# A graph layer on one core: first edges of the later chunks found in pieces in block 5, second sums added in pairs

## The chip, the cores and the metric

The kernel runs on one core of a Trainium2 chip. The metric is the device time of one execution in microseconds (us), the median of several runs. Engines are called as in the profile: PE is TensorE (PEld its weight loads), DVE is VectorE, ACT is ScalarE, POOL is GpSimd, SP is SyncE, which only issues DMAs. L339 is line 339 of the kernel before.

## The reference

One layer of a graph network on 6250 nodes with 64 features and 206250 edges, sorted by destination. Each node's features are normalized and clipped at zero; each edge's message is its source's row plus the edge's own 64 features; messages are summed by destination; an MLP follows, and the node's input is added.

```python
h = jnp.maximum(_layernorm(x, axis=-1), 0.0)
msg = h[src] + edge_feat                       # 206250 x 64
agg = jax.ops.segment_sum(msg, dst, num_segments=6250)
out = x + relu(agg @ W1 + b1) @ W2 + b2
```

## The kernel before

The two halves of the message are summed in different ways.

**The h half.** `h` is held in SBUF (`h2`). Three nodes make a window; each window takes up to 128 edges. Per window (a "tile"), `count` (L838) makes on PE, from one-hots that DVE prepares (`rows_of_tiles`, L823; every second call begins with `encode`, L808), a table of how often each source occurs for each of the window's nodes; ACT copies it to `ring` (L852). `products` (L858) multiplies `h2` with that table over 49 pieces, and `add_products` (L890) adds the result to the sums `agg` on DVE. Six tiles are a step, 14 steps a block of 84 tiles or 252 nodes; there are 22 blocks and 311 steps. A block's products run in steps 1 to 8 of the next block (`FRESH` is 9), and its sums are added in step 9. Some nodes' windows hold more than 128 edges; 14 further tiles ("second tiles") at the end of block 3 hold the rest. Their results, in `tail`, are added by `add_seconds` (L900) at places that are known only at run time: a group of node numbers is loaded into DVE registers, and then each is added on its own (L907). Once all are in, the MLPs of blocks 0 to 3 become ready (`ready`).

**The edge half.** Edge features are summed by chunks of 42 nodes. A chunk starts at the edge that is its first node's first; `chunk_starts` (L318) finds these with small matmuls (L324), `chunk_rows` (L327) turns them into numbers from which SP's loads take their addresses, `chunk_columns` (L333) adds the starts of four quarters on DVE (L339, `quarters`) and turns them into columns with matmuls against a one (L345), and `chunk_index` (L348) copies these out as a gather's indices. Then, for each group `t` of 32 chunks, POOL gathers the destinations (`fetch_dst`, L359), DVE makes them relative to the chunk (`chunk_nodes`, L363; L367 and L368), and PE and ACT turn them (`chunk_turn`, L371; L375 and L376) into `rel`. From it `chunk_hot` makes one-hots (L418), `chunk_sum` sums the edges into `bank` (L429), and `chunk_place` (L453) adds them to the block's products. There are 132 chunks in 5 groups; groups 0 and 1 are used from the start on, group 2 from block 10 on.

**The last 24 groups of 1024 edges** get their h rows from a table in DRAM: POOL gathers them one column at a time and adds them to the loaded edge features (`pfeat`), in a queue with planned costs (`pool_until`, L975); an urgent gather is put at its head. `features_h` (L981) then sums them.

**Order.** The instructions of each engine stand in the order in which the program issues them: the loop over steps (L1121) first runs what the table `before` (L1016) has for step n, then `count`, the one-hots of the next three steps when n mod 3 is 1, products, sums, second sums, an MLP if one is ready (its hidden layer L934 and L936, its product L942 two steps later, its sum L947 a step after that), and last what `later` and `turns` hold. The codes of the windows are unpacked in four steps (L655 to L674) and turned by `turn` (L680). PSUM tiles with the tag "po" share one buffer: `pstart`, `pcols`, `pdst`, the `pw` of `turn`, `ph` and `po` of the MLPs, and `over` of two checks at step 100 (L769). Each has to wait until the one before it has been read. `dstq`, shared by the gathered destinations and `quarters`, has two.

Until now the later chunks' first edges (chunks 64 to 131) are worked out at steps 64 to 71, where also the second sums are added, at steps 66 to 69 in groups of 4, 4, 4 and 2; the gathers for groups 2, 3 and 4 are issued at steps 72, 76 and 80, made relative 8 steps later and turned 9 steps later.

Of the kernel before, what the change touches and what calls it, by code (L numbers as in the profile page):

```python
# [10 lines left out]
F32 = mybir.dt.float32  # L11
# [11 lines left out]
P = 128  # L23
# [42 lines left out]
NX = 14  # L66
# [3 lines left out]
SB = 3  # L70
ST = 6
STEPS = BT // ST

FRESH = 9
# [12 lines left out]
NC = NS // CN  # L87
CV = CN // V
assert NC * CN == NS and BN % CN == 0 and CV * V == CN and NX == CV
RC = P // JQ  # L90
NT = -(-NC // RC)
# [28 lines left out]
def gnn_kernel(ctx: ExitStack, tc: tile.TileContext, x, src_t, dst_t, dst_g, edge, w1, b1, w2, b2, out):  # L120
# [195 lines left out]
    known = {}  # L316
# [10 lines left out]
    def chunk_rows(c0, c1):  # L327
        px = known.pop(("s", c0))
        s = starts[:, c0:c1]
        nc.vector.tensor_scalar(s, px[:1, :c1 - c0], float(G * P * J - CE), None, op0=OP.min)  # L330
        nc.vector.tensor_copy(starts_i[:, c0:c1], s)

    def chunk_columns(t0, t1, tag="po", bufs=1):  # L333

        px = ps.tile([P, NT + 1], F32, tag=tag, name="pcols", bufs=bufs)
        n = (t1 - t0) * RC
        assert n <= JP * RC
        quarters = late.tile([P, JP * RC, JQ], F32, tag="dstq", bufs=2, name="quarters")[0:1, :n]
        nc.vector.tensor_tensor(quarters, starts[:, t0 * RC:t1 * RC].unsqueeze(2).to_broadcast([1, n, JQ]),  # L339
                                row_e.unsqueeze(1).to_broadcast([1, n, JQ]), op=OP.add)  # L340
        rows = [(t, quarters[:, (t - t0) * RC:(t - t0 + 1) * RC, :]) for t in range(t0, t1)]
        if t0 == 0:
            rows.append((NT, row_n))
        for t, of in rows:
            nc.tensor.matmul(px[:, t:t + 1], of.rearrange("o c q -> o (c q)"), ones[0:1, 0:1], start=True, stop=True)  # L345
        known["t", t0] = px
# [61 lines left out]
    def load(u):  # L408
        for k in range(GB):
            load_chunk(u, k)  # L410
# [476 lines left out]
    hids.append(hots_p[0][:, :BN])  # L887
    spare["hotp"] = [a.rearrange("p (j w) -> p j w", j=J) for a in hots_p]

    def add_products(b):  # L890
        pv = pvs.pop(b)
        n = nodes(b)
        for a, z, c in at_columns(b, 0, n):
            to = agg[:, start[b] + a:start[b] + z]
            nc.vector.tensor_tensor(to, to, pv[:, c:c + z - a], op=OP.add)  # L895
        if b == SB:
            for a, z, c in at_columns(b, n, n + NX * V):
                nc.vector.tensor_copy(tail[:, a - n:z - n], pv[:, c:c + z - a])

    def add_seconds(k):  # L900
        n = min(4, NX - k)
        node = nc.values_load_multi_w_load_instructions(
            second_n[0:1, k:k + n], engines=[mybir.EngineType.DVE], min_val=0, max_val=DUMP,
            skip_runtime_bounds_check_because="sums of a node's number and 0, at most DUMP by a min")[1]
        for j in range(n):
            to = agg[:, ds(node[j], V)]
            nc.vector.tensor_tensor(to, to, tail[:, (k + j) * V:(k + j + 1) * V], op=OP.add)  # L907
# [91 lines left out]
        f()  # L999
    chunk_rows(0, 2 * RC)  # L1000
    load(0)
    chunk_columns(0, 2, "pc", 2)
    turn(0, P, columns(0))
    seek(9, 3)
# [7 lines left out]
    for g in range(GA + 2, GA + 4):  # L1012
# [13 lines left out]
        13: [second_flags],  # L1026
        15: [second_ranks],
        17: [second_words],
        64: [lambda: chunk_starts(2 * RC, NC)],
        68: [lambda: chunk_rows(2 * RC, NC), lambda: chunk_columns(2, NT)],  # L1030
        71: [lambda: chunk_index(2, NT)],
        100: [lambda: outside(0), lambda: outside(1)],
        (NW - 1) * STEPS + 8: [limits],
        (NW - 1) * STEPS + 9: [limits_found],
# [30 lines left out]
    unpack_later(n - 4, lambda: unpack(2 * PC, 1, NX, second_b, NX))  # L1065
    turns.setdefault(n, []).append(lambda: turn(2 * PC, NX, [(0, NX, SX)]))
    for t in range(1, NT):
        n = 18 if t == 1 else 64 + 4 * t
        before.setdefault(n, []).append(lambda t=t: queue.insert(0, (GATHER_US, lambda: fetch_dst(t))))
        n = 32 if t == 1 else n + 8  # L1070
        before.setdefault(n, []).append(lambda t=t: chunk_nodes(t))
        before.setdefault(n + 1, []).append(lambda t=t: chunk_turn(t))
# [48 lines left out]
    for n in range(NSTEP):  # L1121
        b, s = block_of(n)
        for f in before.get(n, []):
            f()
        count(n)
        if n % (HT // ST) == 1 or n == 0:
            rows_of_tiles(n // (HT // ST) + 1) if n else None
        if b and 1 <= s < FRESH:
            products(b - 1, PART[s], PART[s + 1])
        if b and s == FRESH:  # L1130
            add_products(b - 1)
            if b - 1 > SB:
                ready.append(b - 1)
        if b - 1 == SB and s > FRESH and (s - FRESH - 1) * 4 < NX:
            add_seconds((s - FRESH - 1) * 4)
            if (s - FRESH) * 4 >= NX:
                ready[:0] = range(SB + 1)
        if s in (2, 9) and ready:
            mlp(ready.pop(0), n)
        for f in later.pop(n, []) + turns.pop(n, []):  # L1140
            f()
        if n >= 3:
            if s in (5, 11) and h_next < G and fetched.get(min(h_next + 1, G - 1), 1e9) + LAND_US <= clock(n):
                features_h(h_next)
                h_next = min(h_next + GB, G)
                add_later(n + 3)
            if n == 3:
                pool[0] = clock(n - 1) + OPENING_US
            pool_until(clock(n) + LAND_US)
# [144 lines left out]
```

## Time and profile before

| | before |
|---|---|
| median of 3 runs | 504.35 us (502.35 to 505.71) |
| profiled execution | 503.97 us |
| its span, first to last instruction | 502.3 us |
| mean granted PE clock | 0.943 |
| PE busy | 429.1 us (85%) |
| DVE, ACT, POOL busy | 354.3, 351.8, 374.1 us |

The span and the busy times are of the profiled execution. Busy shares are means over stages with different limits; step 64 lies at about 135 us and step 72 at about 150 us of the span, steps 77 to 89 between 157 and 178 us, and steps 97 to 105 between 188 and 203 us.

### The profile page before, as it was taken

Reading aid. Unit: us, or ns where it says so; the run is one execution under the profiler, and the core shown is the slowest. Engines: PE = TensorE matmul, PEld = TensorE weight load, DVE = VectorE, ACT = ScalarE, POOL = GpSimd, SP = SyncE. Lnnn points to the kernel's source line nnn. Section 1 sums busy time; section 2 is a strip of 40 time slices with the busy share of each in tenths; the row PEclk is TensorE's granted clock in tenths of the full one; section 3 lists DMA queues with packets and bytes.
Section 4 is the critical chain, followed back from the end, with each engine's and each line's share of the span. In section 5 each row is a group of like instructions: output and inputs, shape, how many; then the busy total and the mean of one; then the engine's idle time right before and its main releaser. Section 6 shows DMA issues by size and latency. Waiting matters only on the chain.

```text
span 502.3 us, 17233 instructions
## 1 busy us (share of the span) xinstructions
PE 429.1 (85%) x7194; PEld 374.7 (75%) x7195; DVE 354.3 (71%) x776; ACT 351.8 (70%) x517; POOL 374.1 (74%) x260
## 2 busy tenths in 40 slices
PE   3023799998879998999999999999998999999984
PEld 3023688877768788888788888888887888888864
DVE  4799858977588765787758757787666686677721
ACT  3628978687556767768688778778776677677650
POOL 6866848888887788888888888888888888885000
PEclk9556779999989998999999999999998999999998
DMA  8849637587465665857658758659658568567310
GB/s 225 238 130 301 142 72 190 135 198 174 115 154 127 170 148 133 191 139 187 162 119 211 170 127 217 156 122 246 149 134 216 102 148 204 129 154 168 107 38 15
DMA packets 113355, 78.65 MB, mean 157 GB/s; under 512 B 32736, under 2 KB 108632, under 8 KB 113048
## 3 DMA queue, kind: packets, MB, share of 16 engines
q1 hardware_dynamic: 84356, 65.87, 45.0%
q0 software_dynamic: 28624, 10.11, 17.1%
q10 hardware_dynamic: 292, 1.52, 0.9%
q8 instruction: 58, 0.95, 0.8%
q14 instruction: 25, 0.20, 0.1%
HBM read 73.48 MB, written 3.99 MB: 154 GB/s over the span
## 4 chain that ended last, share of the span: by engine, by line
PE 53%; ACT 14%; DVE 11%; POOL 10%; issue 6%; DMA 5%; DVEq 0%; POOLq 0%; ACTq 0%
PE pv L864 20%; PE pc L846 17%; POOL pfeat L283 9%; ACT ring L852 8%; PE bank L429 6%; DMA pfeat<-table,src_p 4%; DVE hot L832 2%; PE bank L486 2%; PE po L942 2%; ACT kq L695 2%; PE pv L459 2%; PE ph L934 1%; ACT kv L699 1%; DMA firsts_i<-in_dst_g 1%; PE pk L688 1%
## 5 line engine op out<-in xcount | busy, mean ns | idle before, releaser
L283 POOL DMA_INDIRECT pfeat<-table,src_p x188 | 325.9, 1734 | 60.7 <-issue 51.5
L852 ACT ACTIVATE ring<-pc 128x882 fp32r<-128x882 f32 x310 | 276.7, 924 | 82.1 <-PE pc L846 70.4
L846 PE MATMUL pc<-hot 128*128 128x147 fp8e4 x1862 | 178.4, 234 | 25.2 <-ACT ring L852 13.5
L832 DVE TENSOR_TENSOR hot<-at,of 128x576 int32<-128x576 bf16 x208 | 163.2, 826 | 41.4 <-PE pc L846 30.6
L864 PE MATMUL pv<-ring,h 128*128 128x252 f32 (+1 forms) x1078 | 171.3, 296 | 0.8 <-ACT ring L856 0.8
L846 PEld LDWEIGHTS <-hot 128*128 128x128 fp8e4 x1862 | 128.7, 101 | 49.4 <-issue 21.8
L864 PEld LDWEIGHTS pv<-ring,h 128*128 128x128 f32 x1078 | 140.5, 192 | 1.2 <-ACT ring L856 1.0
L429 PE MATMUL bank<-feat,hotf 128*18 128x64 f32 x3168 | 73.5, 225 | 3.1 <-issue 2.0
L429 PEld LDWEIGHTS bank<-feat,hotf 128*18 128x18 f32 x3168 | 49.2, 99 | 21.6 <-issue 4.8
L895 DVE TENSOR_TENSOR sums<-sums,pv 128x252 f32<-128x252 f32 (+4 forms) x34 | 10.0, 323 | 52.8 <-PE pv L864 37.6
L418 DVE TENSOR_TENSOR hotf<-rel,iota 128x432 f32<-128x432 bf16 (+1 forms) x67 | 39.8, 595 | 0.0
L695 ACT ACTIVATE kq<-pk 128x512 bf16<-128x512 f32 (+18 forms) x48 | 18.4, 449 | 12.8 <-PE pk L688 10.2
L813 DVE TENSOR_TENSOR at<-iota_a,kq 128x576 bf16<-128x576 bf16 (+1 forms) x52 | 23.5, 452 | 0.5
L936 ACT ACTIVATE after<-ph,b1s 128x252 f32<-128x252 f32 (+3 forms) x26 | 12.0, 469 | 15.3 <-PE ph L934 14.0
L283 POOL DMA_INDIRECT sums<-in_dst_g,row_i x15 | 17.4, 1162 | 7.0 <-issue 4.3
L819 DVE TENSOR_TENSOR of<-of,kv 128x432 bf16<-128x432 bf16 (+1 forms) x52 | 20.0, 385 | 3.3 <-DVE of L813 0.5
L283 POOL DMA_INDIRECT words<-packed,first_i x15 | 17.7, 1181 | 4.6 <-issue 4.0
L947 DVE TENSOR_TENSOR after<-po,after 126x128 f32<-126x128 f32 (+3 forms) x26 | 7.5, 288 | 18.1 <-PE po L942 18.1
L934 PE MATMUL ph<-sums,w1s 128*128 128x252 f32 (+3 forms) x52 | 17.1, 417 | 3.1 <-issue 1.8
L813 DVE TENSOR_TENSOR of<-iota_w,kq 128x432 bf16<-128x432 bf16 (+1 forms) x52 | 19.5, 374 | 0.0
L324 PE MATMUL pstart<-begins,first 128*1 128x9 f32 (+2 forms) x30 | 1.6, 172 | 17.2 <-DVE sums L509 9.3
L942 PE MATMUL po<-w2s,after 128*126 128x64 f32 (+3 forms) x104 | 15.9, 278 | 0.2 <-issue 0.2
(183 smaller groups left out, 315.6 us busy)
## 6 DMA issues: line engine op xcount, KB each, us to landing
feat<-in_edge SPq DMA_DIRECT2D x132, 384.0 KB
pfeat<-in_edge SPq DMA_DIRECT2D x23, 256.0 KB
pfeat<-table,src_p POOLq DMA_INDIRECT x188
out_y<-after SPq DMA_DIRECT2D x23, 63.0 KB
dstn<-in_dst_g SPq DMA_DIRECT2D x1, 1024.0 KB
table<-xl SPq DMA_DIRECT2D x2, 512.0 KB
after<-in_x SPq DMA_DIRECT2D x4, 252.0 KB
packed<-dstn ACTq DMA_DIRECT2D x1, 768.0 KB
```

The lines of the kernel that those rows point to most:

```text
L283: nc.gpsimd.indirect_dma_start(out=rows, out_offset=None, in_=source, in_offset=bass.IndirectOffsetOnAxis(ap=index, axis=0), compute_op=op)
L418: nc.vector.tensor_tensor(hot_of[u][:, :n].rearrange("p c j w -> p (c j) w"), rel[:, c:c + n].rearrange("p c q k -> p (c q k)").unsqueeze( ...
L429: nc.tensor.matmul(bank[q * QP:q * QP + WQ, at:at + D], hot_of[u][:, c, j, :], feats[u][c][:, j, :], start=(k == 0), stop=(k == JP - 1))
L695: nc.scalar.activation(kq[:, q, at:at + n].rearrange("s i k o -> s (i k) o"), pk[:, q, a:a + n].rearrange("s i k -> s (i k)").unsqueeze(2) ...
L813: nc.vector.tensor_tensor(to[:, :n].rearrange("s i k (m o) -> s (i k) m o", o=2), iota_k.rearrange("s (m o) -> s m o", o=2).unsqueeze(1).t ...
L819: nc.vector.tensor_tensor(pairs_of, pairs_of, kv[:, c:c + n].rearrange("s i k o -> s (i k) o").unsqueeze(2) .to_broadcast([P, 2 * n, WE // ...
L832: nc.vector.tensor_tensor(hot[:, :n, c:c + m * A8].rearrange("s i (w a) -> s i w a", a=A8), at[:, o:o + n, k].unsqueeze(2).to_broadcast([P ...
L846: nc.tensor.matmul(pc[:, k, q * K:(q + 1) * K], hot[:, i, :P], hot[:, i, P:P + K], start=True, stop=True)
L852: nc.scalar.activation(to.rearrange("p h (k m) -> p h k m", k=2), pc[:, :, :ST // 2 * K].rearrange("p k (m h) -> p h k m", h=HI), AF.Copy)
L864: nc.tensor.matmul(pvs[b], h2[:, h, :], ring[:, h, c:c + columns_of_block(b)], start=(h == 0), stop=(h == HI - 1))
L934: nc.tensor.matmul(ph[:, :n], w1s, agg[:, start[b]:start[b + 1]], start=True, stop=True)
L942: nc.tensor.matmul(po[:pairs[b], k, :], hid[:, k:2 * pairs[b]:2], w2s, start=True, stop=True)
```

## The change

The later chunks' first edges are worked out 13 steps later and in more pieces: `chunk_starts` at step 77, `chunk_rows` at 79, the quarters (now a function of their own) at 80, the columns' matmuls at 83, the index at 85. The gathers move by 16 steps, to 88, 92 and 96, with what follows them (relative at 96, 100, 104; turned at 97, 101, 105). The second sums are added two at a time in the seven steps 66 to 72. For the first two groups of chunks, in the opening, quarters and columns are still called one after the other.

```diff
-    def chunk_columns(t0, t1, tag="po", bufs=1):
-
-        px = ps.tile([P, NT + 1], F32, tag=tag, name="pcols", bufs=bufs)
+    def chunk_quarters(t0, t1):
         n = (t1 - t0) * RC
         assert n <= JP * RC
         quarters = late.tile([P, JP * RC, JQ], F32, tag="dstq", bufs=2, name="quarters")[0:1, :n]
         nc.vector.tensor_tensor(quarters, starts[:, t0 * RC:t1 * RC].unsqueeze(2).to_broadcast([1, n, JQ]),
                                 row_e.unsqueeze(1).to_broadcast([1, n, JQ]), op=OP.add)
+        known["q", t0] = quarters
+
+    def chunk_columns(t0, t1, tag="po", bufs=1):
+
+        px = ps.tile([P, NT + 1], F32, tag=tag, name="pcols", bufs=bufs)
+        quarters = known.pop(("q", t0))
...
+    SECONDS = [(SB + 1) * STEPS + FRESH + 1 + k for k in range(-(-NX // 2))]
+
...
     def add_seconds(k):
-        n = min(4, NX - k)
+        n = min(2, NX - k)
...
     load(0)
+    chunk_quarters(0, 2)
     chunk_columns(0, 2, "pc", 2)
...
-        64: [lambda: chunk_starts(2 * RC, NC)],
-        68: [lambda: chunk_rows(2 * RC, NC), lambda: chunk_columns(2, NT)],
-        71: [lambda: chunk_index(2, NT)],
+        77: [lambda: chunk_starts(2 * RC, NC)],
+        79: [lambda: chunk_rows(2 * RC, NC)],
+        80: [lambda: chunk_quarters(2, NT)],
+        83: [lambda: chunk_columns(2, NT)],
+        85: [lambda: chunk_index(2, NT)],
...
     for t in range(1, NT):
-        n = 18 if t == 1 else 64 + 4 * t
+        n = 18 if t == 1 else 80 + 4 * t
...
-        if b - 1 == SB and s > FRESH and (s - FRESH - 1) * 4 < NX:
-            add_seconds((s - FRESH - 1) * 4)
-            if (s - FRESH) * 4 >= NX:
+        if n in SECONDS:
+            k = SECONDS.index(n)
+            add_seconds(2 * k)
+            if 2 * k + 2 >= NX:
                 ready[:0] = range(SB + 1)
```

## The prediction

> **What bounds the kernel now.** I read the page first, then the list of waits, then the timelines of TensorE and VectorE around the moved pieces, and last the busy time by stretches.
>
> ```profile
> span 502.3 us, 17233 instructions
> PE 429.1 (85%) x7194; PEld 374.7 (75%) x7195; DVE 354.3 (71%) x776; ACT 351.8 (70%) x517; POOL 374.1 (74%) x260
> ```
>
> TensorE is the fullest engine, and most of its idle time lies in the opening. What a change is worth is therefore the TensorE time that it takes out of the chain or puts into it. The timeline of TensorE shows where the change starts (steps 64 to 72; each group of L846 is one step's count; in brackets stand the idle time before a row and its releaser):
>
> ```profile
> 135.31 0.40 PE L324 MATMUL pstart<-begins,first 128*1 128x10 f32 x10
> ...
> 136.76 0.30 PE L846 MATMUL pc<-hot 128*128 128x147 fp8e4 x2
> ...
> 138.35 0.56 PE L846 MATMUL pc<-hot 128*128 128x147 fp8e4 x6
> ...
> 143.99 0.88 PE L345 MATMUL pcols<-ones,quarters 1*128 1x1 f32 x6 [3.17 <-DVE quarters L339]
> 144.80 0.92 PE L846 MATMUL pc<-hot 128*128 128x147 fp8e4 x6
> ...
> 151.09 0.69 PE L934 MATMUL ph<-sums,w1s 128*128 128x252 f32 x2
> ```
>
> L324 (step 64) is the matmul of the first edges, and L345 (step 68) that of the index columns. L345 stands idle for 3.17 us, because `quarters` on VectorE is queued behind everything in this view:
>
> ```profile
> 139.12 0.44 DVE L895 TENSOR_TENSOR sums<-sums,pv 128x162 f32<-128x162 f32 x2 [3.98 <-PE pc L846]
> ...
> 139.70 0.76 DVE L907 TENSOR_TENSOR sums<-sums,after 128x3 f32 x4
> 140.37 1.57 DVE L832 TENSOR_TENSOR hot<-at,of 128x576 int32<-128x576 bf16 x2
> 141.86 0.74 DVE L907 TENSOR_TENSOR sums<-sums,after 128x3 f32 x4
> 142.52 0.60 DVE L418 TENSOR_TENSOR hotf<-rel,iota 128x432 f32<-128x432 bf16 x1
> ...
> 143.87 0.73 DVE L907 TENSOR_TENSOR sums<-sums,after 128x3 f32 x4
> 145.19 0.36 DVE L907 TENSOR_TENSOR sums<-sums,after 128x3 f32 x2 [0.59 <-issue]
> 145.46 0.45 DVE L813 TENSOR_TENSOR at<-iota_a,kq 128x576 bf16<-128x576 bf16 x1
> ...
> 146.73 1.58 DVE L832 TENSOR_TENSOR hot<-at,of 128x576 int32<-128x576 bf16 x2
> ...
> 148.36 0.68 DVE L926 TENSOR_TENSOR after<-after,b2s 126x512 f32<-126x512 f32 x1
> ```
>
> VectorE itself waited until 139.12 for the products of step 64, and only then works off the sums of block 3, two groups of second sums, the one-hots of steps 67 to 69 and the small pieces. The pause also costs clock, as the busy time by stretches shows (the last three columns are granted clock, DMA share and GB/s):
>
> ```profile
> 141.21:144.63 3.42, 0.64 (x6) 0.64 (x6) 3.14 (x13) 0.91 (x1) 2.83 (x2) 1.00 0.83 226
> 144.63:148.04 3.41, 3.41 (x62) 2.56 (x61) 2.68 (x7) 1.51 (x2) 2.80 (x3) 0.50 0.22 29
> 192.41:195.83 3.42, 1.62 (x20) 1.36 (x16) 0.33 (x1) 3.33 (x9) 2.81 (x3) 1.00 0.51 119
> 195.83:199.24 3.41, 3.41 (x21) 3.32 (x20) 1.77 (x3) 1.51 (x2) 2.88 (x2) 0.50 0.16 14
> 117.32:120.73 3.41, 1.89 (x60) 1.37 (x60) 3.27 (x8) 2.64 (x3) 2.80 (x3) 1.00 0.70 178
> 120.73:124.15 3.42, 3.25 (x57) 2.90 (x58) 3.39 (x7) 2.77 (x5) 3.12 (x2) 1.00 0.85 215
> ```
>
> After a stretch with 0.64 us of TensorE work the next one runs at clock 0.50; so it does after one with 1.62 us, and not after one with 1.89 us. A count takes 0.92 instead of 0.56 us there (144.80 against 138.35), so one such stretch loses about 3.41 x (1 - 0.56 / 0.92) = 1.3 us.
>
> **Term 1, steps 64 to 72.** The change takes L324 and L345 out of this stretch and spreads the second sums over steps 66 to 72. Without L324 everything from step 64 on comes 136.76 - 135.31 = 1.45 us earlier: L895 starts at 137.67. From there the chain is VectorE's. Since an MLP reads sums that any second sum may touch, the hidden layer of block 0 (L934, step 72) now has to wait for the last group, which is issued in step 72 too; before, the last group was over at 145.55, long ahead of 151.09. The chain, by the rows: L895 with its copy 0.58 (139.12 to 139.70); two sums 0.27 (145.19 to 145.46); one-hots 1.49 (140.37 to 141.86); two sums 0.27; L418 0.60; two sums 0.27 (step 68); 0.59 for a register load with nothing ahead of it, and two sums 0.27 (step 69); encoding and one-hots 2.85 (145.46 to 148.31, step 70); two sums 0.27; 0.59 and two sums 0.27 (step 71); L926 0.68 and the last two sums 0.36 (step 72). Together 9.36, so the sums end at 147.03 and L934 starts at about 147.05: **4.0 us earlier** than 151.09. TensorE does not get there first: count 68 would be over at 139.8, its chunk's matmuls wait for L418 until 140.9, count 72 waits for the one-hots until 144.9, and L934 for the sums. One wait of 3.17 becomes three of about 1.1, 0.9 and 0.7, in two stretches, each with over 1.89 us of work left; I take the clock as full. Bounds: seven groups instead of four mean three more loads. If no load showed, TensorE alone would gain another 2.7 (the three waits), 6.7 in all; if all seven showed, five more than I count, the gain would be 4.0 - 5 x 0.59 = 1.1. I take 4.0, since loads that have a long instruction ahead of them (140.37, 143.87) show no idle time in the rows.
>
> **Term 2, the pieces that come back.** L324 returns at step 77, in a stretch dense with products: +1.45. L345 returns at step 83 at full clock: 0.88 x 0.56 / 0.92 = +0.5. The three small VectorE pieces between L418's end (143.12) and 143.87 return at steps 79 and 80, where the node pieces of chunk group 2 have just left; these were longer, so that costs nothing. If that cover were gone it would be 0.75. There is one more wait: `pstart` and the turn's `pw` share one PSUM buffer, so the turn at step 77 has to wait until L330, at the head of step 79, has read `pstart`.
>
> ```profile
> 158.60 0.60 DVE L418 TENSOR_TENSOR hotf<-rel,iota 128x432 f32<-128x432 bf16 x1
> 159.12 1.57 DVE L832 TENSOR_TENSOR hot<-at,of 128x576 int32<-128x576 bf16 x2
> ...
> 159.38 0.31 PE L689 MATMUL pw<-identb,code 128*128 128x128 bf16 x1
> ```
>
> L418 is of step 78 and L832 of step 79, so VectorE is at L330's place at 159.12; the turn's L689 comes at 159.38 and with L324 ahead of it at 160.8. Cost nothing, with 1.6 us to spare.
>
> **Term 3, the transposes.** They go from steps 81, 85, 89 to 97, 101, 105, and their gathers by the same 16 steps on POOL's queue, where nothing but each other waits for them so far from their use in block 10.
>
> ```profile
> 164.09 0.61 PE L375 MATMUL pdst<-shift,dstq 128*128 128x128 f32 x3
> ...
> 175.59 0.61 PE L375 MATMUL pdst<-shift,dstq 128*128 128x128 f32 x3 [0.39 <-DVE after L947]
> ```
> ```profile
> 166.25 0.41 DVE L367 TENSOR_SCALAR dstq<-dstq,cols 128x384 f32<-128x384 int32 x1
> 166.70 0.62 DVE L368 SCALAR_TENSOR_TENSOR dstq<-iota_q,cols,dstq 128x384 f32<-128x384 int16 x1
> ```
>
> Leaving: 3 x 0.44 (0.61 less the overlap with what follows) and the wait of 0.39: -1.7. Arriving, they meet a stretch that is worse:
>
> ```profile
> 186.95 3.42 ACT L852 ACTIVATE ring<-pc 128x882 fp32r<-128x882 f32 x4 [0.50 <-PE po L942]
> ...
> 195.12 0.47 ACT L936 ACTIVATE after<-ph,b1s 128x252 f32<-128x252 f32 x1
> ```
> ```profile
> 187.01 0.29 DVE L947 TENSOR_TENSOR after<-po,after 105x128 f32<-105x128 f32 x1
> 187.21 1.57 DVE L832 TENSOR_TENSOR hot<-at,of 128x576 int32<-128x576 bf16 x2
> ```
> ```profile
> 187.91 0.55 PE L846 MATMUL pc<-hot 128*128 128x147 fp8e4 x6 [0.24 <-issue]
> ...
> 194.39 0.69 PE L934 MATMUL ph<-sums,w1s 128*128 128x252 f32 x2 [1.80 <-issue]
> 194.92 0.55 PE L846 MATMUL pc<-hot 128*128 128x147 fp8e4 x6
> ```
>
> At step 97 the transposes stand ahead of count 97 (187.91) and need the one PSUM buffer that L947 of step 96 frees; L947 now comes 1.03 later (L367 and L368 go ahead of it), ends at 188.33, and with 0.44 of transposes count 97 starts at 188.8: 0.9 late. ScalarE, which is full from 186.95 to 195.59, would take up count 97 at 188.7 and takes it at 189.45: +0.8, and this reaches L934 of step 100, which already waits 1.80 us for ScalarE to free the same buffer. At step 101 the next transposes stand ahead of count 101 (194.92) and must wait for L936's end at 195.59: +0.7 and +0.44. At step 105: +0.44, no wait. Sum **+2.4**. Bounds: 0.4 (only step 105 shows, the rest disappears into the 1.80 us), and 7.2 (three node pieces on VectorE 3.1, transposes 1.3, the two waits 1.5, one more slow stretch 1.3).
>
> The Trainium skill, page "TensorE: Matmul & The Clock Gate", section "Why this matters for your kernels", asks for no TensorE idle gaps above about 3 us between bursts. By that rule 3.17 would cost clock and neither the 1.80 us at step 100 nor anything I add there could. This trace disagrees: 1.80 us of idle time in one stretch was followed by 0.50. By the rule the sum would be the same, since I count that slow stretch before and after.
>
> **The sum.** -4.0 + 1.45 + 0.5 - 1.7 + 2.4 = -1.35. The profiled execution took 503.97 us (502.3 of it the span); it becomes 502.6. It lies 0.38 below the median of the runs shown, so the median becomes 504.35 - 1.35 = **503.0**.
>
> **Rivals.**
>
> *Block 6 hides the transposes.* Term 3's arrivals fall to 0.4, and with the pauses cut up no stretch falls below 1.89 us of work, so that the slow one after 195.83 goes as well: -1.35 - 2.0 - 1.3 = -4.65, 499.7. For it: L934 waits anyway. Against it: the wait is for ScalarE, and the delayed count 97 feeds ScalarE.
>
> *The loads show.* All seven groups pay 0.59: +2.95, 506.0, slower than before. It decides from the third of the five additional loads on (1.35 / 0.59 = 2.3). For it: three more loads, and groups of two leave less work to cover the next. Against it: in steps 66 to 68, 70 and 72 something long stands ahead.
>
> *Block 6 takes it back.* The wait at L375 of step 97 and 101 becomes the bound, with its upper price of 7.2 instead of 2.4: 503.0 + 4.8 = 507.8, slower. It decides from 3.8 us of cost in steps 96 to 102 on. For it: ScalarE's and VectorE's rows there have no gaps, and one slow stretch is already tripped. Against it: VectorE ends that work early, 0.33 us in 192.41 to 195.83.
>
> *The wait does not go.* Step 68's wait may only change its name, from L339 to L418 and L907; that is counted in term 1 and in the loads.
>
> **How the numbers follow.** Forecast 0.43, block 6 hides 0.17, loads show 0.2, block 6 takes it back 0.2. The forecast's own range is 501 to 505. From 499.0 to 507.6 the rivals are in, but for the far half of the last one and what lies beyond the first. About 1%, or 5 us, is what a measurement of this kernel tells from no change. Faster by that needs under 499.3: half of the first rival (0.085) and a twelfth of the forecast, 0.12. Slower by that needs over 509.4: a third of the last rival and a quarter of the one of the loads, 0.12. Within it 0.76.
>
> **What would show it.** Right: no wait of L345 above 0.3 us; L934 of step 72 released by L907, some 4 us earlier; clock 1.00 from 141 to 150; L324 at step 77 taking 1.4 us; L375 at steps 97 and 101 idle 0.5 us or more, released by L947 and L936. Wrong: idle times of 0.59 before most pairs of L907; a slow stretch between 138 and 150; L689 of step 77 waiting; step 101 at the same time as before or later although step 90 came 4 us earlier.

## The result and the profile after

The changed kernel took 507.93 us in the median of 16 runs (504.34 to 510.47), against 501.9 us in the median of the kernel before beside it (16 runs, one of them at 666.24). The ratio is **1.0109, 95% interval 1.0081 to 1.0137**: slower by about 1%, where 503.0 and no change were forecast. The profiled execution took 508.43 us, 506.7 of it the span.

```profile
span 506.7 us, 17240 instructions
PE 432.4 (85%) x7194; PEld 376.5 (74%) x7195; DVE 354.4 (70%) x776; ACT 352.5 (70%) x517; POOL 371.3 (73%) x260
```

The work of the engines is the same, and the span is 4.4 us longer. What the change set out to do did happen. TensorE's timeline in steps 72 to 83 (idle time before a row and its releaser in brackets):

```profile
146.44 0.56 PE L850 MATMUL pc<-hot 128*128 128x147 fp8e4 x6 [0.72 <-DVE hot L836]
...
149.07 0.69 PE L940 MATMUL ph<-sums,w1s 128*128 128x252 f32 x2 [1.08 <-DVE sums L913]
...
155.23 0.55 PE L324 MATMUL pstart<-begins,first 128*1 128x10 f32 x16
155.71 0.56 PE L850 MATMUL pc<-hot 128*128 128x147 fp8e4 x6
...
164.10 0.82 PE L349 MATMUL pcols<-ones,quarters 1*128 1x1 f32 x6 [0.22 <-DVE after L953]
```

The wait of 3.17 us at L345 is gone (L349 waits 0.22), the hidden layer of step 72 (L940) is held by the second sums (L913) as foreseen, and the stretches from 141 on run at clock 1.00:

```profile
141.21:144.63 3.42, 2.81 (x71) 2.08 (x70) 2.66 (x11) 2.92 (x4) 3.11 (x2) 1.00 0.91 247
144.63:148.04 3.41, 2.63 (x34) 2.19 (x31) 2.35 (x8) 3.01 (x4) 2.80 (x3) 1.00 0.96 259
```

Then TensorE's timeline around the transposes' new place (steps 92 to 101):

```profile
180.72 0.45 PE L433 MATMUL bank<-feat,hotf 128*18 128x64 f32 x13 [0.25 <-issue]
...
183.17 0.32 PE L433 MATMUL bank<-feat,hotf 128*18 128x64 f32 x5 [0.49 <-issue]
183.89 0.33 PE L433 MATMUL bank<-feat,hotf 128*18 128x64 f32 x6 [0.41 <-issue]
...
186.29 0.61 PE L379 MATMUL pdst<-shift,dstq 128*128 128x128 f32 x3
...
191.04 0.55 PE L850 MATMUL pc<-hot 128*128 128x147 fp8e4 x6 [1.02 <-issue]
...
195.03 1.21 PE L940 MATMUL ph<-sums,w1s 128*128 128x252 f32 x2 [2.43 <-ACT over L775]
196.80 0.91 PE L379 MATMUL pdst<-shift,dstq 128*128 128x128 f32 x3 [0.56 <-ACT after L942]
197.50 0.95 PE L850 MATMUL pc<-hot 128*128 128x147 fp8e4 x6
```

Three short stops on "issue" (nothing in the profile held TensorE), and a fourth of 0.20 us at 185.35, come ahead of the first transposes, and one of 1.02 us behind them; the wait at step 100, 1.80 before, is 2.43; the transposes of step 101 wait 0.56 for L942 and then take 0.91 instead of 0.61. The busy time by stretches shows why (TensorE's busy time behind the length; granted clock third from the end):

```profile
187.97:191.38 3.41, 2.39 (x29) 2.29 (x27) 2.91 (x6) 1.95 (x4) 2.80 (x3) 1.00 1.08 345
191.38:194.79 3.41, 1.21 (x20) 0.96 (x17) 0.28 (x1) 3.32 (x11) 2.80 (x3) 1.00 0.47 113
194.79:198.20 3.41, 2.61 (x12) 1.85 (x12) 0.00 (x0) 1.91 (x5) 2.80 (x3) 0.50 0.22 19
198.20:201.61 3.41, 3.41 (x21) 3.32 (x19) 2.09 (x3) 1.87 (x3) 2.80 (x3) 0.50 0.17 15
```

Two slow stretches follow, where the kernel before had one.

To place the time I took, from each trace, the moment at which ScalarE starts to read the counts of a step (L856; L852 before), one such moment per step. The table gives the us from one step to another; in brackets stands the number of slow stretches (3.41 us each at a granted clock of 0.50) in steps 96 to 105. Letters name the chips; the first comparison's chip is not known. Kernels marked * were profiled in a run well above their kernel's usual time, and their totals are not used; the ratios leave such runs out, the medians hold every run.

| kernel | chip | 57–73 | 80–96 | 96–105 | 105–126 | 132–150 | 174–204 | span |
|---|---|---|---|---|---|---|---|---|
| before | – | 26.1 | 23.9 | 15.1 (1) | 29.8 | 27.5 | 42.1 | 502.3 |
| after | – | 22.9 | 24.7 | **20.0** (2) | 29.5 | 28.9 | 45.7 | 506.7 |
| c1_pairs_only | A | 24.6 | 24.1 | 13.5 (0) | 30.0 | 26.9 | 42.4 | 501.1 |
| c2_edges_only | A | 22.6 | 23.4 | **17.4** (1) | 29.9 | 26.8 | 43.2 | 501.3 |
| c3_after_checks60 | A | 24.8 | 24.8 | **17.4** (1) | 29.8 | 27.8 | 48.2 | 507.2 |
| c4_before_checks60 | A | 25.0 | 23.4 | 12.9 (0) | 29.9 | 26.9 | 43.2 | 502.6 |
| c0_after_again | B | 22.1 | 21.7 | **19.5** (2) | 27.9 | 26.5 | 41.3 | 492.1 |
| c5_gathers92 | B | 22.1 | 21.8 | 15.4 (1) | 29.9 | 26.5 | 41.3 | 494.1 |
| c6_gathers80_alone | B | 26.2 | 20.7 | **18.1** (1) | 27.9 | 26.5 | 41.3 | 496.7 |
| c7_edges57 * | B | 26.5 | 22.7 | 15.3 (1) | 27.9 | 26.5 | 41.3 | 501.3 |
| d0_before_again * | C | 24.8 | 23.4 | 14.3 (0) | 29.2 | 32.1 | 47.3 | 508.4 |
| d1_gathers92_again | C | 24.9 | 22.0 | 15.1 (1) | 31.5 | 27.2 | 41.8 | 502.6 |
| d2_gathers80_alone_again | C | 26.2 | 21.8 | **16.6** (0) | 29.8 | 26.9 | 42.6 | 504.9 |
| d3_edges57_again | C | 25.7 | 24.0 | 13.5 (0) | 29.8 | 26.9 | 41.8 | 500.1 |
| e0_after_third | D | 23.5 | 24.0 | **18.3** (1) | 29.9 | 28.2 | 43.1 | 503.6 |
| e1_gathers92_third * | D | 24.2 | 22.1 | 15.1 (1) | 32.1 | 30.2 | 41.9 | 507.3 |
| e2_before_half_piece | D | 25.0 | 24.0 | 13.5 (0) | 29.9 | 26.9 | 41.8 | 501.5 |
| e3_after_half_piece | D | 23.6 | 23.5 | **20.5** (2) | 29.6 | 28.9 | 45.0 | 508.0 |
| f0_before_delay10 | B | 24.2 | 23.0 | 13.8 (0) | 30.1 | 26.5 | 41.3 | 489.0 |
| f1_before_delay20 | B | 25.6 | 22.7 | 15.3 (1) | 32.2 | 26.5 | 41.2 | 493.0 |

Bold are the eight kernels with transposes at 97, 101 and 105. In the pair of the first comparison the changed kernel wins 3.2 us in steps 57 to 73, loses 4.9 in 96 to 105, 1.4 in 132 to 150 and 3.7 in 174 to 204. By step 204 it is 8.5 us behind, and by step 310 4.3, since the kernel before has stops of its own in between (1.80 us at 383).

### The profile page after: what moved, and what is told of

It reads as the page before. It is cut to its first block, busy times and chain, and to the rows that moved or that the text cites. A ratio compares the mean times of both kernels' runs of the same rounds, so it can differ in the third digit from the quotient of the medians.

```text
span 506.7 us, 17240 instructions
## 1 busy us (share of the span) xinstructions
PE 432.4 (85%) x7194; PEld 376.5 (74%) x7195; DVE 354.4 (70%) x776; ACT 352.5 (70%) x517; POOL 371.3 (73%) x260
## 4 chain that ended last, share of the span: by engine, by line
PE 67%; ACT 15%; DVE 12%; issue 4%; DMA 2%; DVEq 0%; ACTq 0%
PE pv L868 24%; PE pc L850 22%; ACT ring L856 9%; PE bank L433 8%; DVE hot L836 3%; PE bank L490 3%; PE ph L940 2%; PE po L948 2%; ACT kq L699 2%; PE pv L463 2%; ACT kv L703 1%; DMA feat<-in_edge 1%; PE pk L692 1%; DMA firsts_i<-in_dst_g 1%; DVE xl L541 1%
## 5 line engine op out<-in xcount | busy, mean ns | idle before, releaser
L856 ACT ACTIVATE ring<-pc 128x882 fp32r<-128x882 f32 x310 | 276.8, 924 | 83.8 <-PE pc L850 68.7
L850 PE MATMUL pc<-hot 128*128 128x147 fp8e4 x1862 | 178.4, 234 | 28.0 <-ACT ring L856 15.1
L850 PEld LDWEIGHTS <-hot 128*128 128x128 fp8e4 x1862 | 128.7, 101 | 52.5 <-issue 23.5
L433 PEld LDWEIGHTS bank<-feat,hotf 128*18 128x18 f32 x3168 | 48.8, 98 | 22.6 <-issue 4.3
L699 ACT ACTIVATE kq<-pk 128x512 bf16<-128x512 f32 (+18 forms) x48 | 18.3, 444 | 12.8 <-PE pk L692 10.8
L942 ACT ACTIVATE after<-ph,b1s 128x252 f32<-128x252 f32 (+3 forms) x26 | 12.0, 470 | 17.9 <-PE ph L940 16.2
L817 DVE TENSOR_TENSOR at<-iota_a,kq 128x576 bf16<-128x576 bf16 (+1 forms) x52 | 23.5, 452 | 0.5
L940 PE MATMUL ph<-sums,w1s 128*128 128x252 f32 (+3 forms) x52 | 17.6, 428 | 4.4 <-ACT over L775 2.4
L324 PE MATMUL pstart<-begins,first 128*1 128x9 f32 (+2 forms) x30 | 1.4, 172 | 16.2 <-issue 8.9
```

What stands on the lines that cost most here:

```text
L433: nc.tensor.matmul(bank[q * QP:q * QP + WQ, at:at + D], hot_of[u][:, c, j, :], feats[u][c][:, j, :], start=(k == 0), stop=(k == JP - 1))
L699: nc.scalar.activation(kq[:, q, at:at + n].rearrange("s i k o -> s (i k) o"), pk[:, q, a:a + n].rearrange("s i k -> s (i k)").unsqueeze(2) ...
L817: nc.vector.tensor_tensor(to[:, :n].rearrange("s i k (m o) -> s (i k) m o", o=2), iota_k.rearrange("s (m o) -> s m o", o=2).unsqueeze(1).t ...
L850: nc.tensor.matmul(pc[:, k, q * K:(q + 1) * K], hot[:, i, :P], hot[:, i, P:P + K], start=True, stop=True)
L856: nc.scalar.activation(to.rearrange("p h (k m) -> p h k m", k=2), pc[:, :, :ST // 2 * K].rearrange("p k (m h) -> p h k m", h=HI), AF.Copy)
L940: nc.tensor.matmul(ph[:, :n], w1s, agg[:, start[b]:start[b + 1]], start=True, stop=True)
```

## The experiments

Kernels c1 to c4 ran on chip A, beside 29 runs of the kernel before (503.15 us median). Their expectations set four theories against each other: COLLISION (the moved pieces meet ScalarE's backlog and the one PSUM buffer in steps 96 to 102; in its narrow form, they meet the checks of step 100), LOADS (the register loads of the pairs), SUPPLY (TensorE's instructions come too late there, since the moved matmuls shift what each load of code holds) and SPREAD (node pieces and transposes cost 2 to 4 us in any place there).

**c1_pairs_only**: the kernel before with the second sums in pairs (steps 66 to 72) and nothing else.

```diff
-        n = min(4, NX - k)
+        n = min(2, NX - k)
...
-        if b - 1 == SB and s > FRESH and (s - FRESH - 1) * 4 < NX:
+        if n in SECONDS:
```

> The kernel before with the second sums in pairs at steps 66 to 72; the first edges stay at 64 to 71 and the transposes at 81, 85, 89. Theory COLLISION (the loss arises in steps 96 to 102, where the moved node pieces and transposes meet ScalarE's backlog and the one PSUM buffer): nothing moves there, so no loss; the pairs shorten VectorE's chain ahead of the quarters by four sums, about 0.8 us, but the hidden layer of block 0 waits for the last pair; 1 us faster to 1 us slower than before, and from step 92 to 105 the same pace as before. Rival LOADS (three more register loads and the new wait at step 72 cost the time): 2 to 5 us slower, visible by step 74.

Measured: 503.02 us, ratio 1.001 (0.9981 to 1.0038). The pairs cost and bring nothing that shows. LOADS falls.

**c2_edges_only**: the changed kernel with the sums by fours again (the reverse of the diff above).

> The changed kernel with the second sums again by fours at steps 66 to 69; first edges at 77 to 85, gathers at 88, 92, 96. COLLISION: the whole loss is here, 4 to 7 us slower than before, and it arises between steps 91 and 105; by step 91 it is 3 to 6 us ahead. LOADS: this is faster than before by 3 us or more.

Measured: 507.9 us in 6 runs, which lie at 503 to 506 and at 510 to 511; ratio 1.0103 (1.0053 to 1.0153). So the loss comes with the moved edges and transposes.

**c3_after_checks60** and **c4_before_checks60**: the checks `outside` from step 100 to 60, in the changed kernel and in the one before.

```diff
-        100: [lambda: outside(0), lambda: outside(1)],
+        60: [lambda: outside(0), lambda: outside(1)],
```

> The changed kernel with the two checks of step 100 (outside 0 and 1, 1.3 us of ScalarE, both through the one PSUM buffer) moved to step 60. COLLISION in its narrow form (the checks are what the late transposes collide with): the hidden layer of step 100 no longer waits 2.4 us, no slow clock after it, 4 us or more faster than the changed kernel, about level with before or faster. Rival SUPPLY (TensorE's instructions come too late in steps 92 to 100, since the moved matmuls shift what each load of code holds): still 4 us or more slower than before, with idle times put down to issue at 180 to 192 us. Rival SPREAD (node pieces and transposes cost in any place there): 2 to 4 us slower than before.

> The kernel before with the same two checks at step 60: the control for the last kernel. It has a wait of 1.8 us at step 100 and a slow stretch after it. COLLISION in its narrow form: 2 to 3 us faster than before (1.8 and 1.3 of clock), so that the last kernel has to be compared with this one. SUPPLY and SPREAD: the same wait goes here, 1 to 3 us faster.

Measured: c3 507.34 us, ratio 1.005 (1.0018 to 1.0081); c4 503.78 us, 1.0002 (0.9972 to 1.0032). Without the checks there the changed kernel still needs 17.4 us for steps 96 to 105, and the kernel before 12.9. The checks are at most a part of it, and COLLISION in its narrow form falls. By the ratio c3 lies within SPREAD's 2 to 4 us. Its trace has the stops on "issue" that SUPPLY expected (2.4 us from 178 to 192.5), but c2's has 0.6 and the same 17.4 us. No theory had c4 unchanged; all expected it 1 to 3 us faster.

The next four ran on chip B, beside 35 runs of the kernel before. PLACE is the theory that the transposes' place is the cause; LAG, that being ahead by step 73 is taken back wherever TensorE runs short.

**c0_after_again**: the changed kernel, no edit.

> The changed kernel once more, for a second profile. PLACE (the transposes of L379, now at steps 97, 101 and 105, stand among the checks, the MLP and the sums of block 6, and block 6 pays for them there): 507 to 508.5, with 5 to 8 us lost again between the evacuations of steps 91 and 105, and no loss that comes back in the same place later. LAG (what is won by step 73 puts TensorE ahead of the gathers and of its own instruction stream, and that is taken back at whatever stage is short of supplies): 507 to 508.5 as well, but the loss stands in other places than in the first profile.

**c5_gathers92**: transposes at 109, 113 and 117.

```diff
-        n = 18 if t == 1 else 80 + 4 * t
+        n = 18 if t == 1 else 92 + 4 * t
```

> The changed kernel with the three fetches, rankings and transposes of the later chunks 12 steps later still: transposes at steps 109, 113 and 117, the same places of a block that before had them at (81, 85, 89 are 28 steps earlier), and none of them beside the checks of step 100. PLACE: the loss between steps 91 and 105 falls from 7.7 us to 1 or less, the gain at 81 to 89 stays; 501 to 503. LAG: 4 us or more are lost between steps 91 and 117 all the same; 505 to 508.

**c6_gathers80_alone**: the kernel before with transposes at 97, 101 and 105 and nothing else.

```diff
-        n = 18 if t == 1 else 64 + 4 * t
+        n = 18 if t == 1 else 80 + 4 * t
```

> The kernel before with nothing changed but the fetches, rankings and transposes 16 steps later (transposes at 97, 101, 105); first edges at 64 to 71 and the sums by fours as before. PLACE: no gain at steps 64 to 72, -1.7 us by step 91, then 5 to 8 us lost by step 105; 506 to 509. LAG: nothing is won before, so there is nothing to take back: within 1 us of before at step 105 and in the time, 502 to 504.

**c7_edges57**: the changed kernel with the edges in block 4 and the transposes where they were before.

```diff
-        77: [lambda: chunk_starts(2 * RC, NC)],
-        79: [lambda: chunk_rows(2 * RC, NC)],
-        80: [lambda: chunk_quarters(2, NT)],
-        83: [lambda: chunk_columns(2, NT)],
-        85: [lambda: chunk_index(2, NT)],
+        57: [lambda: chunk_starts(2 * RC, NC)],
+        59: [lambda: chunk_rows(2 * RC, NC)],
+        60: [lambda: chunk_quarters(2, NT)],
+        62: [lambda: chunk_columns(2, NT)],
+        64: [lambda: chunk_index(2, NT)],
...
-        n = 18 if t == 1 else 80 + 4 * t
+        n = 18 if t == 1 else 64 + 4 * t
```

> The changed kernel with the five pieces of the first edges earlier instead of later (steps 57, 59, 60, 62 and 64, in block 4, where no MLP holds the buffer po), and the fetches and transposes where they were before (transposes at 81, 85, 89). Sums in pairs. PLACE: 3 to 4 us are won by step 73 and kept; 499 to 501, the best of all. LAG: won by step 73 and taken back between steps 91 and 105 or later; 503 to 507.

Measured, all beside 497.31 us for the kernel before: c0 496.81, ratio 1.0015 (0.9973 to 1.0057); c5 496.39, 1.0012 (0.9982 to 1.0043); c6 496.76, 1.0015 (0.9978 to 1.0052); c7 494.93, 0.9967 (0.9928 to 1.0005). **On this chip the change costs nothing**, and no theory had foreseen that. Yet in the trace the loss of steps 96 to 105 is there: 19.5 us in c0 and 18.1 in c6, 15.4 in c5.

Two things differ on chip B. TensorE never waits on "issue": after 58 us no row there has more than 0.15 us of it, while such rows add up to 3.5 to 7.4 us in the profiles on A, C and D. The list of TensorE's waits from 100 to 480 us, of the changed kernel in the first comparison:

```profile
PE pc L850 <- ACT ring L856: 7.6, 14, 1.0
PE pc L850 <- DVE hot L836: 3.3, 4, 1.6
PE pc L850 <- issue: 2.4, 6, 1.0
PE ph L940 <- ACT over L775: 2.4, 1, 2.4
PE bank L433 <- issue: 2.0, 6, 0.5
PE bank L490 <- issue: 1.3, 2, 0.9
```

and the same list of c5 on chip B:

```profile
PE bank L490 <- DMA pfeat<-table,src_p: 4.6, 3, 2.2
PE pc L850 <- ACT ring L856: 4.3, 6, 1.0
PE pc L850 <- DVE hot L836: 3.3, 4, 1.6
PE ph L940 <- ACT over L775: 1.8, 1, 1.8
```

And TensorE there catches up with the gathers on POOL, which run one behind the other from 45 us on: near the end it waits for the last of them. TensorE and POOL of c6:

```profile
461.05 0.31 PE L486 MATMUL bank<-after,pfeat 128*64 128x42 f32 x2 [0.38 <-DMA pfeat<-table,src_p]
463.70 0.31 PE L486 MATMUL bank<-after,pfeat 128*64 128x42 f32 x2 [2.34 <-DMA pfeat<-table,src_p]
```
```profile
458.77 2.08 POOL L283 DMA_INDIRECT pfeat<-table,src_p  x1 [0.30 <-issue]
```

In c5, c6 and c7 TensorE waits 2.7 to 4.6 us like this. What is lost around step 100 would then shorten that wait, and the order fits: c5, c6 and c0 need 15.4, 18.1 and 19.5 us for steps 96 to 105 and wait 4.6, 2.7 and 0.2 us for gathers.

The third group ran on chip C (before: 502.94 us, 35 runs). STARVE is the theory that the loss is tied to the chips with "issue" waits and to when TensorE arrives, not to the transposes.

**d0_before_again** (no edit), **d1_gathers92_again**, **d2_gathers80_alone_again** and **d3_edges57_again** (the edits of c5, c6 and c7).

> The kernel before once more, for a second profile of it. The last four kernels ran on a chip where everything took 497 us instead of 503 and no profile showed TensorE idle on 'issue' after the opening; the earlier ones, all at 501 to 508, showed 5 to 7 us of such idle time. STARVE (the idle time called 'issue' belongs to the chip, and the change costs 1% only where it exists): if this chip shows 'issue' waits, 502 to 505 us; if not, 495 to 499 us, and its evacuations then stand within 1 us of the same kernel with late transposes from step 120 on. PLACE (the cost is in the transposes' place, whatever the chip): the same time as the before of this call, and nothing more is expected of it.

> The changed kernel with transposes at steps 109, 113, 117, once more, in the hope of the slower chip. PLACE: no slower than before on either chip (ratio 0.995 to 1.002). STARVE: 1.000 where TensorE shows no 'issue' waits, and 1.005 to 1.012 where it does, as the changed kernel itself, since it is the early arrival and not the transposes that meets those waits.

> The kernel before with the transposes alone at 97, 101, 105, once more. PLACE: slower by 0.8 to 1.2% where the changed kernel is. STARVE: 1.000 (0.997 to 1.003) on either chip, since nothing is won ahead of step 73 that could shift TensorE against its supplies.

> First edges at steps 57 to 64, transposes as before, sums in pairs, once more; its profile there was a disturbed one. PLACE: 0.992 to 0.998 on either chip, the gain of 3 to 4 us kept. STARVE: 0.997 where there are no 'issue' waits (as measured), 1.003 to 1.010 where there are.

Measured: d0 503.38 us, 1.0008 (0.9983 to 1.0033); d1 502.97, 1.0013 (0.9984 to 1.0041); d2 505.26, **1.0049 (1.0021 to 1.0077)**; d3 505.18, 1.0056 (1.0029 to 1.0084). d1 and d2 speak for PLACE against STARVE: moved alone, the transposes lose half a per cent (less than the 0.8 to 1.2% that PLACE had, more than STARVE's 0.3%), and moved on to 109 they lose nothing that shows, though being ahead by step 73 is kept; LAG, which expected no change from d2's edit and a loss from that of c5 and d1, falls. d3 speaks against PLACE and lies in STARVE's range (1.003 to 1.010): it should have won 3 to 4 us and lost half a per cent. Its profiled execution took 501.78 us, so the trace doesn't hold that loss, but it shows that the edges won nothing in block 4 (25.7 us for steps 57 to 73): TensorE waits there for the turn of step 56 to leave the same PSUM buffer.

```profile
126.41 0.54 PE L324 MATMUL pstart<-begins,first 128*1 128x10 f32 x16 [2.70 <-ACT kv L703]
```

The fourth group ran on chip D (before: 503.27 us, 31 runs).

**e0_after_third** (the changed kernel), **e1_gathers92_third** (c5's edit), and **e2_before_half_piece** and **e3_after_half_piece**: the kernel before and the changed one, with 128 more instructions in TensorE's program.

```diff
         px = ps.tile([P, GN], F32, tag=tag, name="pstart", bufs=bufs)
+        for i in range(64 if c0 == 0 else 0):
+            nc.tensor.matmul(px[:1, 0:1], onesb[:, 0:1], onesb[:, 0:1], start=True, stop=True)
```

> The changed kernel, beside its version with later transposes on the same chip. PLACE: 1.008 to 1.012 where 'issue' waits show, 1.000 to 1.003 where not. STARVE: the same; this run is the yardstick for the next three.

> Transposes at steps 109, 113, 117. PLACE: 0.6% or more below the changed kernel of this call wherever that one is slow. STARVE (the place of the transposes is not it): within 0.3% of it.

> The kernel before with 64 more 1x1 bf16 products on TensorE (128 instructions with their weight loads) ahead of its first pstart products, where TensorE waits 9.3 us for VectorE, so that every later instruction stands 128 places further in TensorE's program, half of a 16 KB piece at 64 bytes each. Their results are overwritten. PLACE: the same time as before within 0.3%, the 1.8 us stalls in the same steps. STARVE: the stalls move to other steps, and the time moves by 0.4 to 1% one way or the other where 'issue' waits show; nothing where they don't.

> The changed kernel with the same 128 instructions ahead. PLACE: as slow as the changed kernel of this call, within 0.3%. STARVE: its loss changes by 0.4% or more, since the stalls fall elsewhere than at 180 to 195 us.

Measured: e0 508.04 us, **1.0091 (1.0056 to 1.0126)**; e1 506.03, 1.0014 (0.9973 to 1.0055); e2 502.87, 0.9991 (0.9959 to 1.0022); e3 508.24, 1.0065 (1.0025 to 1.0104). The loss repeats on a second chip. The shift of the program moves neither kernel by more than its interval, so STARVE and SUPPLY, as places in the program, find no support. Beside e0, the later transposes of e1 take most of the loss away by the ratio; by the medians it is 2 of the 4.8 us, and e1's 12 runs lie anywhere from 500.4 to 509.0, so the size stays loose. In d1 and e1 the transposes cost some 2 us where they now stand (31.5 and 32.1 us for steps 105 to 126, against 29.2 to 29.9 in the other kernels of C and D).

The last two ran on chip B again (before: 497.71 us, 17 runs). They hold the kernel before up on purpose.

**f0_before_delay10** and **f1_before_delay20**: 10 and 20 products of 128x512 at step 106, read by nobody.

```diff
+    def hold_up():
+        held = ps.tile([P, 512], F32, tag="po", name="held", bufs=1)
+        for _ in range(10):
+            nc.tensor.matmul(held, identb, rel.rearrange("p c q k -> p (c q k)")[:, :512], start=True, stop=True)
+
+    before.setdefault(106, []).append(hold_up)
```

> The kernel before with ten idle 128x512 bf16 products on TensorE at step 106 (2 to 4 us of work whose result nobody reads). COMPOUND (arriving late brings on the losses near 252 and 312 us): what is lost by step 120 is 2 to 3 us, the time 2 us slower in some runs and 6 to 8 us in others. SIMPLE (the held-up time is all that is lost): 1.004 to 1.006. SLACK (TensorE has room there): under 1.002.

> The same with twenty products (4 to 8 us). COMPOUND: 8 us or more above before in most runs (1.016 or more), with stalls on 'issue' near 252 to 260 and 312 to 320 us in the profile. SIMPLE: the hold-up as the profile shows it by step 120, and no more. SLACK: 1.004 or less.

Measured: f0 493.06 us, **0.9909 (0.9875 to 0.9942)**; f1 495.16, 0.9939 (0.9909 to 0.9968). Held up by 2.33 and 4.49 us of work, the kernel is faster.

```profile
199.28 2.33 PE L1041 MATMUL held<-rel,identb 128*128 128x512 bf16 x10
```
```profile
200.81 4.49 PE L1041 MATMUL held<-rel,identb 128*128 128x512 bf16 x20
```

Neither SIMPLE nor COMPOUND holds here, and SLACK, whose bounds are kept, foresaw no gain: the hold-up does show where it stands (count 106 is read 2.2 and 4.3 us later than in c0, measured from step 105), and the time comes back at the end. In both profiles the last gather ends 2.6 to 7.5 us earlier than in c0, c5 and c6 (at 455.4 and 453.4, against 458.0 to 460.9), and TensorE doesn't wait for it. Why the gathers come sooner is not shown. COMPOUND is not settled either, since this chip has no "issue" waits. f0 beats both kernels on chip B; on the other chips it was not tried.

## Why the prediction was wrong

**The wait of step 68** went as predicted, with the right releaser in its place and, in the pair, full clock from 141 to 150. (In c3, d1, e0 and e1 a slow stretch begins between 148 and 152 us all the same; these need 23.5 to 24.9 us for steps 57 to 73, the other five with the edges at 77 need 22.1 to 23.6.) Its price was mis-sized. By step 73 the pair of profiles shows 3.2 us won (26.1 against 22.9) where term 1 had 4.0, and 3.2 is itself too much: the profile on which the sum was made had a longer wait than most of its siblings. L345's row in c4, d0 and d2, all with the edges of before:

```profile
144.28 0.82 PE L345 MATMUL pcols<-ones,quarters 1*128 1x1 f32 x6 [2.59 <-DVE quarters L339]
```
```profile
145.48 0.82 PE L345 MATMUL pcols<-ones,quarters 1*128 1x1 f32 x6 [2.53 <-DVE quarters L339]
```
```profile
145.21 0.82 PE L345 MATMUL pcols<-ones,quarters 1*128 1x1 f32 x6 [3.13 <-DVE quarters L339]
```

In d2, as in the first profile, stops on "issue" break up L324's products ahead of it; in the other seven it is 2.0 to 2.6. Over all nine profiles with the edges of before (25.3 us on the mean for steps 57 to 73) and all nine with the edges at 77 (23.4), 1.9 us are won. Register loads showed twice (0.57 each), as counted, and once more with 0.28.

**The pieces that come back** were over-sized, 1.3 us against 1.95: L324 takes 0.48 us of the path (155.23 to 155.71), not 1.45, which had been read from rows with idle time in them, and L349 took 0.82 where 0.5 was put down.

**The transposes** are the step that failed. Leaving steps 81 to 89 won 1.9 us (d2's 21.8 for steps 80 to 96 against 23.7 on the mean of d0 and d3), near the 1.7 predicted. Arriving, the eight kernels with transposes at 97 to 105 need 16.6 to 20.5 us for steps 96 to 105, 18.5 on the mean; the other twelve in the table 12.9 to 15.4, 14.4 on the mean. No two overlap. That is **4.1 us where +2.4 was put down**, and 4.9 in the pair of profiles, inside the bounds of 0.4 to 7.2. The two waits were named rightly, in place and releaser, though the first doesn't show in the changed kernel's first profile, where TensorE comes late to step 97; c0 has both. TensorE, then ScalarE of c0:

```profile
184.63 0.61 PE L379 MATMUL pdst<-shift,dstq 128*128 128x128 f32 x3 [0.87 <-DVE after L953]
...
193.04 0.91 PE L379 MATMUL pdst<-shift,dstq 128*128 128x128 f32 x3 [0.56 <-ACT after L942]
193.75 0.95 PE L850 MATMUL pc<-hot 128*128 128x147 fp8e4 x6
```
```profile
185.28 0.49 ACT L380 ACTIVATE rel<-pdst 128x384 bf16<-128x384 f32 x1 [1.05 <-PE pdst L379]
185.66 1.87 ACT L856 ACTIVATE ring<-pc 128x882 fp32r<-128x882 f32 x2
...
192.52 0.47 ACT L942 ACTIVATE after<-ph,b1s 128x252 f32<-128x252 f32 x1 [0.21 <-PE ph L940]
193.99 0.49 ACT L380 ACTIVATE rel<-pdst 128x384 bf16<-128x384 f32 x1 [1.00 <-PE pdst L379]
194.73 0.92 ACT L856 ACTIVATE ring<-pc 128x882 fp32r<-128x882 f32 x1 [0.25 <-PE pc L850]
```

Beside c5, the same kernel with the transposes 12 steps later on the same chip, the term can be read step by step: the two traces keep the same pace to 0.01 us from step 90 to 96. Then c0 falls behind by 1.3 us up to count 100 (0.8 in the working), by another 2.1 with count 101 (1.14), 0.35 up to count 104 (nothing) and 0.44 with count 105 (0.44), together 4.2. At step 97 TensorE waits for VectorE, whose two node pieces took 1.20 us (183.09 to 184.29) and not 1.03.

At step 101 it is the clock. In both traces the wait at step 100 is followed by a slow stretch, from 191.89 in c0 and from 189.33 in c5. In c0 the transposes and count 101 fall into it and take 0.91 and 0.95 instead of 0.61 and 0.55, so that from L942's start to the reading of count 101 it is 2.21 us (192.52 to 194.73), in c5 0.39 (188.84 to 189.23). And the 0.56 us that the transposes wait for L942 leave that slow stretch with 2.85 us of work, and a second slow one follows; in c5 it is full of work, and the next one runs at 1.00. The busy time of the two stretches, c0's and then c5's (TensorE's behind the length):

```profile
191.89:195.30 3.41, 2.85 (x15) 2.20 (x14) 0.57 (x1) 1.95 (x4) 2.80 (x3) 0.50 0.19 29
```
```profile
189.33:192.75 3.42, 3.42 (x21) 3.33 (x20) 1.99 (x3) 1.72 (x2) 2.50 (x4) 0.50 0.15 38
```

So term 3 failed at a slow stretch that it put at nothing: it counted one before and after, and a second one (1.3) stood in the upper bound alone. At the same number of slow stretches the late transposes cost 3.0 us (none: 16.6 against 13.6 on the mean) or 2.6 (one: 17.8 against 15.2), near the 2.4. Three of the changed kernel's four profiles (first, c0, e0, e3) have two, and there it is 20.0; the five of the kernel before (first, d0, e2, f0, f1) have one or none. ScalarE's reading of the transposes (L380, 0.49 us) has no part in c0: count 97 is read 0.04 us after its end (185.07 + 0.55), and at step 101 ScalarE waits 0.25 us for the count.

**The sum again.** With these sizes it is not -1.35 but -1.9 + 0.5 + 0.8 - 1.9 + 4.1 = +1.6 us: the sign turns, but the ratio stands for 5.5. Read whole, steps 57 to 105 take 77.9 us on the mean of the changed kernel's four profiles (75.0 to 79.2) and 74.3 on that of the five with the order of before up to there (first, d0, e2, f0, f1; 72.2 to 76.8): 3.6 us. The prediction's own sign of being wrong is there too: in the pair, count 90 is read 3.9 us earlier than before and count 101 3.0 us later. What is lost after step 105 stays open.

**The rival "Block 6 takes it back"** named the place, the sign and nearly the time (507.8), with a chance of 0.2. That the number fits is luck in part: it was counted from 504.35 us, and the kernel before took 501.9 beside the changed one. It also put the whole price in steps 96 to 102. By step 105 the pair of profiles is 2.5 us apart from step 57 on (79.2 against 76.8); of the 4.4 us in the span 1.2 were there at step 57, ahead of every moved piece; 4.8 come between steps 105 and 204, and 4.1 go again after that. Two stops in between are in no part of the prediction. The changed kernel near 252 and 312 us:

```profile
251.09 1.17 PE L490 MATMUL bank<-after,pfeat 128*64 128x42 f32 x23 [0.86 <-issue]
252.67 0.65 PE L490 MATMUL bank<-after,pfeat 128*64 128x42 f32 x9 [0.40 <-issue]
```
```profile
311.44 0.27 PE L433 MATMUL bank<-feat,hotf 128*18 128x64 f32 x2 [0.42 <-issue]
312.91 0.23 PE L850 MATMUL pc<-hot 128*128 128x147 fp8e4 x1 [0.34 <-issue]
```

A slow stretch follows each (252.80 and 314.24). The kernel before can have them too: in d0's profile (510.05 us) TensorE stops near 254 us for longer:

```profile
254.63 0.55 PE L846 MATMUL pc<-hot 128*128 128x147 fp8e4 x6 [1.91 <-issue]
```

Among the 14 profiles with stops on "issue" (all but chip B's), the changed kernel, c3, e3 and d0 have stops on "issue" of 0.7 us or more in all between 250 and 255 us, and these four need 45.0 to 48.2 us for steps 174 to 204; the other ten have no such stops and need 41.8 to 43.2. Why the changed kernel meets them more often is open: the run that was to tell fell on chip B.

**What stays open.** The transposes' cost at 97 to 105 is shown, in every trace, on every chip. That it is the 1% is shown only in part: d2 (+0.5%), d1 and e1 (no loss shown) point to it, d3 (+0.6% with the transposes in place) doesn't fit, and on chip B it vanishes. Leaving and arriving together, d2's trace falls only 0.6 us behind d0's from step 80 to 105 (38.3 against 37.7), less than the 2.3 us between its median and that of the kernel before.

## What to carry to other kernels

Work that is moved next to a pause is priced at the clock that follows the pause: look up where the slow stretches lie, and whether a wait that comes along leaves room for one more (here the arrival cost 2.6 to 3.0 us at equal clock, and 4.1 on the mean as it came). Price a wait from several executions when it can be had, since one profile's 3.17 us was 2.0 to 2.6 in seven of eight siblings. And where the difference is about 1%, another chip can take it away: ask which engine sets the end there.

## What the runs showed of the hardware

- The same program took 503 us on three chips and 497 us on a fourth. There, in all six profiles, the stretches from step 126 to 204 agree within 0.1 us, and TensorE never stops on "issue"; on the others it stops for 3.5 to 7.4 us in all, in changing places.
- My limit for the clock, 1.89 us of work in a stretch of 3.41, doesn't hold. In the changed kernel 2.08 and 2.06 us were followed by 0.50 (rows below), and 2.39 by 1.00. In all 20 traces between 80 and 450 us, cut into their own stretches, each of the 27 stretches at full clock with less than 1.64 us of TensorE work was followed by 0.50, none with 2.10 or more was, and between these both occur. A slow stretch with less than 3.0 us of work was followed by another slow one each time (8 of 8).

```profile
249.39:252.80 3.41, 2.08 (x38) 1.71 (x37) 2.08 (x5) 0.46 (x2) 2.80 (x3) 1.00 0.69 182
252.80:256.20 3.40, 3.36 (x61) 2.55 (x64) 3.12 (x8) 2.24 (x4) 2.79 (x3) 0.50 0.94 233
310.83:314.24 3.41, 2.06 (x42) 1.31 (x39) 2.68 (x6) 2.14 (x3) 2.80 (x3) 1.00 0.84 234
314.24:317.65 3.41, 3.41 (x23) 3.41 (x20) 1.85 (x3) 3.23 (x9) 2.80 (x3) 0.50 0.72 177
```

  The Trainium skill, page "TensorE: Matmul & The Clock Gate", section "Why this matters for your kernels", warns of gaps above about 3 us; here a wait of 2.43 stood ahead of two slow stretches, so the measurement decides against that limit. The same wait of 1.8 us at step 100 is followed by a slow stretch in c0, c5 and f1, where it leaves one stretch with 1.6 us of work, and not in f0 and e2, where it is shared by two (2.4 and 2.6 us of work each).
- Idle time that the profile calls "issue" can hide a real releaser: L934 of step 100 waited 1.80 us on "issue" in the first profile, and 1.8 us on ScalarE's checks (over, L771 or L775) in those of c0, c5 and c6.
